# Windowed attention layers on one core: Q and K projected by column tiles and transposed on VectorE

## The chip, the cores and the metric

The kernel runs on one core of one Trainium2 chip. Its engines work side by side, each from its own queue in order: TensorE (PE; PEld is its weight load), VectorE (DVE), ScalarE (ACT), GpSimd (POOL), and SyncE (SP), which issues DMAs here. PE writes to the memory PSUM, in whose banks a tile here takes one or two; the other memory on the core is SBUF. The metric is device time in microseconds (us), lower is better. Two times differ by less than about 0.2% when they can't be told apart by the measurement.

## The reference, cut to what matters

A causal attention block stands first (4 sequences of 512 tokens, width 128, 16 heads of 64), then six layers of local attention, then one feed-forward block with the input of the layers added. The change is in the six layers. Per layer:

```python
q, k, v = jnp.split(x @ Wqkv, 3, -1)          # 16 heads of 64 each
q = l2norm(q) * qs                            # per token and head
k = l2norm(k) * ksc
q = q * cos * scale + rotate_half(q) * sin * scale
k = k * cos * inv + rotate_half(k) * sin * inv
out = local_attention(q, k, v)                # windows of 32, each sees itself and the one before
out = out.transpose(0, 2, 1, 3).reshape(b, n, INNER)
return out @ Wo
```

`rotate_half` swaps the two halves of a head's 64 columns and negates one. Each attention layer is followed by a feed-forward layer (layer norm, two products to 341, gelu gate, product back to 128). All in fp32.

## The kernel before, in words

**Stage one** (0 to about 540 us) is the dense causal attention; its functions are `make_q` to `residual1` (lines 260 to 401), its exponentials L339. The change leaves it alone but for the tables it prepares (`layer_tables`, L168).

**Stage two** is a pipeline over 96 units: 6 layers x 4 sequences x 4 tiles of 128 tokens (`Unit`, L530). One call of `slot(n, ...)` (L893) writes out, by hand and for all engines, the instructions of one step; each engine takes its own in that order. Slot n works on three units: u = n (scores to output), nxt = n+1 (transposes of Q and K) and new = n+2 (projections, rotation, norms). Every fourth slot begins the next sequence (`begin`, L847), and the feed-forward of a finished sequence (`Ffn`, L757) is spread over six slots: shift at n, mean, var and scale of its layer norm at n+1 to n+3, its three chunks with gelu at n+3 to n+5, its output product at n+6. So the slots repeat with period four. The steps that matter here:

- `project` (L535): the 128 tokens of the unit times the 1024 columns of Wq, Wk or Wv: two matmuls of 128x512 (four rows in the profile, since each fp32 matmul is two). Tokens stand on partitions, columns (head by head) along the free axis, in one of three PSUM tiles of two banks, `two0` to `two2`, which `two_t` (L516) hands out in rotation. In slot n Q's comes first, after the scores; K's in two halves; V's late.
- `square` (L549, ACT), `sum_squares` (L553, DVE): the sums of squares per token and head, 128x16 for Q and for K. `inverse_norms` (L580): a maximum with 1e-24 (L582), then `rsqrt` (L78): two integer operations on DVE for a first value (L84, L85) and three Newton steps of four operations on POOL (L87 to L90), on 128x32. `over_norm` (L585, POOL) multiplies Q and K by it.
- `rotate` (L558, DVE): the projection in PSUM times the cosine table (L561) and, with the halves swapped, times the sine table (L567); `add_rotated` (L577, POOL) adds the two.
- `transpose_q`, `transpose_k` (L654, L659): through `transposed` (L645), eight 128x128 PE transposes each into the two one-bank PSUM tiles of `one_t` (L520), copied out by ACT (L652). K's tile has 32 columns ahead of its 128, copied from the unit before by POOL (`carry_k`, L668), for the window that looks back.
- `scores` (L670): the mask as eight bf16 products in 64x32 tiles of PE (L676), then 64 products of 64x32 (L687). DVE takes the maximum over each head's 64 scores (L697) and subtracts it (L699); `exponents` (L703) is one ACT pass of 128x1024.
- `transpose_p`, `times_v` (L707, L712): eight PE transposes, two ACT copies, then 64 products with V (L719), whose extra column of ones gives the denominator; DVE divides (L728, L729). `transpose_o` and `project_out_2` (L736, L741) end the unit in the next slot.
- `v_windows` (L628): ACT copies V from PSUM (L634); SP stores it to DRAM and at once loads it back by windows (`vw`, L641).
- ACT holds one table of functions at a time: gelu needs another than the exponential, so a chunk's slot has a load before the gelu (L792) and one at the slot's end (L981).

Weights of the next layer (`wpart`, 512 KB each) are loaded after their last use (`do_project`, L859).

Of the kernel before, what the change touches and what calls it, by code (L numbers as in the profile page):

```python
# [32 lines left out]
def body(ctx: ExitStack, tc: tile.TileContext, a, out: bass.AP):  # L33
# [27 lines left out]
    hsel = const.tile([P, 2], F32, tag="hsel", name="hsel")  # L61
    nc.vector.memset(hsel, 0.0)
    nc.vector.memset(hsel[0:HD, 0:1], 1.0)
    nc.vector.memset(hsel[HD:P, 1:2], 1.0)
    tabs = const.tile([P, NT, 4, HD], F32, tag="tabs", name="tabs")
# [102 lines left out]
    def layer_tables(i):  # L168

        scales = pre.tile([P, 4 * HD], F32, tag="scales", name="scales")  # L170
        nc.sync.dma_start(out=scales, in_=a["scales"][i : i + 1].to_broadcast([P, 4 * HD]))
        lt = pre.tile([P, NT, 4, HD], F32, tag="lt", name="lt", bufs=2)
        nc.gpsimd.tensor_tensor(
            lt.rearrange("p t f d -> p t (f d)"),
            tabs.rearrange("p t f d -> p t (f d)"),
            scales.unsqueeze(1).to_broadcast([P, NT, 4 * HD]),
            ALU.mult,
        )
        return lt

    with tc.manual_schedule():
# [20 lines left out]
        nc.sync.dma_start(out=tabs, in_=a["tabs"])  # L202

# [209 lines left out]
        for m in range(last):  # L413
# [70 lines left out]
            if b == B - 1 and c == 2 and not odd:  # L484
                start = shifted(0), layer_tables(0)
# [4 lines left out]
    s2a = ps2a = s2b = s2 = ps_one = kT_first = vts = vds = None  # L490
# [44 lines left out]
    def project(u, j, c0=0, c1=2):  # L535
        p = u.p[j] if c0 else two_t(((1, 2, 1), (0, 2, 1), (1, 2, 0))[min(u.n, 2)][j], "ps_proj")
        u.p[j] = p
        for c in range(c0, c1):
            mm(  # L539
                p[:, c, :],  # L540
                lhsT=u.xs[:, u.T * P : (u.T + 1) * P],
                rhs=wpart[j][:, c * 512 : (c + 1) * 512],
                start=True,
                stop=True,
            )
        if c1 == 2:
            u.p[j] = flat(p)
# [4 lines left out]

    def sum_squares(u, j):  # L553
        if j == 0:
            u.ss = small.tile([P, 2 * HEADS], F32, tag="ss", name="ss")
        nc.vector.tensor_reduce(u.ss[:, j * HEADS : (j + 1) * HEADS], heads(u.sq[j]), AX.X, ALU.add)  # L556

    def rotate(u, j, between=()):  # L558
        t0 = u.r[j] = s2a.tile([P, INNER], F32, tag="rot", name="rot", bufs=6)
        lt, pf, half = u.lt, u.p[j], HD // 2  # L560
        nc.vector.tensor_tensor(  # L561
            heads(t0), heads(pf), lt[:, u.T, 2 * j].unsqueeze(1).to_broadcast([P, HEADS, HD]), ALU.mult
        )
        for f in between:
            f()
        t1 = u.t1 = s2a.tile([P, INNER], F32, tag="t1", name="t1", bufs=4)
        nc.vector.tensor_tensor(  # L567
            t1.rearrange("p (h t d) -> p h t d", t=2, d=half),
            pf.rearrange("p (h t d) -> p h t d", t=2, d=half)[:, :, ::-1, :],
            lt[:, u.T, 2 * j + 1]  # L570
            .rearrange("p (t d) -> p t d", t=2)
            .unsqueeze(1)
            .to_broadcast([P, HEADS, 2, half]),
            ALU.mult,
        )

    def add_rotated(u, j):  # L577
        nc.gpsimd.tensor_tensor(u.r[j], u.r[j], u.t1, ALU.add)  # L578

    def inverse_norms(u):  # L580

        nc.vector.tensor_scalar(u.ss, u.ss, 1e-24, None, ALU.max)  # L582
        rsqrt(u.ss, 2 * HEADS, nc.gpsimd)

    def over_norm(u, j):  # L585
        nc.gpsimd.tensor_tensor(  # L586
            heads(u.r[j]),
            heads(u.r[j]),
            u.ss[:, j * HEADS : (j + 1) * HEADS].unsqueeze(2).to_broadcast([P, HEADS, HD]),
            ALU.mult,  # L590
        )
# [8 lines left out]
    def second_step():  # L600

        nonlocal s2b, ps_one, kT_first, vts, vds
# [11 lines left out]
        kT_first = s2b.tile([P, NC, W + P], F32, tag="kT_first", name="kT_first")  # L614
        nc.gpsimd.memset(kT_first[:, :, 0:W], 0.0)
# [7 lines left out]
    def new_kT(u):  # L623
        if u.T == 0:
            return kT_first
        return s2.tile([P, NC, W + P], F32, tag="kT", name="kT", bufs=2)

    def v_windows(u):  # L628


        vt, vd = vts[u.n % 2], vds[u.n // NT % 2]
        src = u.p[2].rearrange("p (c a d) -> p a c d", a=2, d=HD)
        for c in range(2):
            nc.scalar.copy(vt[:, c, :, 0:HD], src[:, c])  # L634
        r0 = u.T * P
        nc.sync.dma_start(out=vd[r0 + W : r0 + W + P], in_=vt.rearrange("p a c d -> p a (c d)"))
        u.vw = s2b.tile([P, NW, NC, HD + 1], F32, tag="vw", name="vw", bufs=2)
        for odd in range(2):
            rows = vd[r0 + odd * W : r0 + odd * W + P].rearrange("(j k) a x -> a k j x", k=2 * W)
            for c in range(2):  # L640
                nc.sync.dma_start(  # L641
                    out=u.vw[c * HD : (c + 1) * HD, odd::2].rearrange("p j c d -> p j (c d)"), in_=rows[c]
                )
# [9 lines left out]

    def transpose_q(u):  # L654
        u.qT = s2b.tile([P, NC, P], F32, tag="qT", name="qT", bufs=1)
        for g in range(2):
            transposed(u.r[0], g, u.qT, 0)

    def transpose_k(u):  # L659
        if u.T == 0:  # L660
            u.kT = new_kT(u)
        for g in range(2):
            transposed(u.r[1], g, u.kT, W)

    def carry_k(u, nxt):
        if nxt is not None:
            nxt.kT = new_kT(nxt)
            nc.gpsimd.tensor_copy(nxt.kT[:, :, 0:W], u.kT[:, :, P : P + W])  # L668

    def scores(u):  # L670
# [13 lines left out]
        for c in range(NC):  # L684
            for j in range(NW):
                for h in range(2):
                    mm(  # L687
                        sc[j * W : (j + 1) * W, h, c * 2 * W : (c + 1) * 2 * W],
                        lhsT=u.qT[h * HD : (h + 1) * HD, c, j * W : (j + 1) * W],
                        rhs=u.kT[h * HD : (h + 1) * HD, c, j * W : (j + 2) * W],  # L690
# [4 lines left out]
        s3 = sc.rearrange("p a (c n) -> p a c n", n=2 * W)  # L695
        mx = small.tile([P, 2, NC], F32, tag="mx", name="mx")
        nc.vector.tensor_reduce(mx, s3, AX.X, ALU.max)  # L697
        u.pr = s2.tile([P, NC, 2, 2 * W], F32, tag="pr", name="pr", bufs=2)
        nc.vector.tensor_tensor(  # L699
            u.pr.rearrange("p c a n -> p a c n"), s3, mx.unsqueeze(3).to_broadcast([P, 2, NC, 2 * W]), ALU.subtract  # L700
        )

    def exponents(u):  # L703
        u.prf = u.pr.rearrange("p c a n -> p (c a n)")
        nc.scalar.activation(u.prf, u.prf, AF.Exp)
# [138 lines left out]
    def follower(u):  # L844
        return units[u.n + 1] if u.T + 1 < NT else None

    def begin(u):  # L847
# [3 lines left out]
        if u.n == 0:  # L851
            xs, lt = start
        else:
            xs = shifted(u.b)
            lt = layer_tables(u.i) if u.b == 0 else units[u.n - 1].lt
        for v in units[u.n : u.n + NT]:
            v.xs, v.lt, v.p = xs, lt, [None] * 3

    def do_project(u, j, c0=0, c1=2):  # L859
        project(u, j, c0, c1)  # L860
        if c1 == 2 and u.b + 1 == B and u.T + 1 == NT and u.i + 1 < L:
            wpart[j] = load_part(u.i + 1, j)

    def first_slot():
# [5 lines left out]
        do_project(new, 0)  # L870
        do_project(new, 1)
# [13 lines left out]
        inverse_norms(new)  # L885
        times_v1(B - 1, NC - 1, 1)
        second_step()
        over_norm(new, 0)
        over_norm(new, 1)
        do_project(new, 2)  # L890
        v_windows(new)

    def slot(n, norm, move, geglu):  # L893

        u, prev, nxt, new = unit(n), unit(n - 1), unit(n + 1), unit(n + 2)
        part[0] = -n % 3
        begin(unit(n + 4))  # L900
        if u:
            scores(u)
        if new:
            do_project(new, 0)
            square(new, 0)
        if u:
            exponents(u)
        while behind:
            behind.pop(0)()
# [3 lines left out]
        for f in norm:  # L913
            f()
# [4 lines left out]

        if new and n >= 0:  # L920
            rotate(new, 0, [lambda: residual(prev)] if prev else ())
            add_rotated(new, 0)
        elif prev:
            residual(prev)
        for f in move:
            f()
        if u and norm:
            transpose_p(u, 0)
        if new:
            do_project(new, 1, 0, 1)  # L930
        if u:
            if not norm:
                transpose_p(u, 0)
            transpose_p(u, 1)
        if new and n == -1:
            rotate(new, 0)
            add_rotated(new, 0)
        if new:
            do_project(new, 1, 1)
            square(new, 1)  # L940
        if n == -1:
            residual1(B - 1, y)
# [3 lines left out]
        while later:  # L946
            later.pop(0)()
        if new:
            sum_squares(new, 0)
# [3 lines left out]
        if nxt:  # L953
            transpose_q(nxt)
        if new:
            do_project(new, 2, 0, 2 if geglu else 1)
        if new and geglu:
            v_windows(new)
        if nxt:
            transpose_k(nxt)  # L960
        if new and not geglu:
            do_project(new, 2, 1)
            v_windows(new)
        if n == -1:
            third_step()
        if nxt:
            carry_k(nxt, follower(nxt))
        if new:
# [204 lines left out]
```

## Time and profile before

| | us |
|---|---|
| three runs | 2180.05, 2181.45, 2177.88; median 2180.05 |
| the profiled execution | 2177.22, of which its span 2175.2 |

The mean granted PE clock is 0.995 of full. Busy time in stretches of the span:

| us from the start | length | PE | DVE | ACT | POOL |
|---|---|---|---|---|---|
| 0 to 590 (stage one, start of stage two) | 590.0 | 570.1 | 389.0 | 353.5 | 296.0 |
| 590 to 1000 | 410.0 | 398.9 | 344.5 | 261.0 | 321.9 |
| 1000 to 1500 | 500.0 | 496.7 | 427.1 | 330.3 | 390.6 |
| 1500 to 2100 | 600.0 | 595.8 | 513.9 | 398.5 | 469.1 |
| 2100 to 2175 (end) | 75.0 | 65.5 | 45.6 | 37.5 | 30.7 |

Costliest groups of stage two, over the whole span (instructions, busy us, mean ns):

| line | what | count | busy | mean |
|---|---|---|---|---|
| L539 PE | projections, 128x512 | 1152 | 569.6 | 602 |
| L649 PE | transposes of Q and K, 128x128 | 1536 | 204.6 | 276 |
| L578 POOL | sum of the rotated parts, 128x1024 | 192 | 454.3 | 2367 |
| L586 POOL | product with the inverse norm, 128x1024 | 192 | 361.8 | 1905 |
| L561, L567, L556 DVE | rotation, sums of squares, 128x1024 | 192 each | 233.8, 233.2, 232.3 | 1217, 1215, 1210 |
| L551 ACT | squares, 128x1024 | 192 | 196.5 | 1024 |

How to read the profile: L539 is line 539 of the kernel. A row of a group has its count, then busy time and mean duration, then the engine's idle time just before the group and what ended most of it. In a timeline a row is start, duration (from the first start to the last end if several are merged, x8), engine, line, operation, output<-inputs; an idle time before it stands in brackets. A matmul's end is modelled and lies past the next one's start; `64*32` are the rows and columns of PE that it uses. "issue" is a wait for nothing that the profile shows.

### The profile page before, as it was taken

The page shows a single profiled execution, that of the slowest core. Times are in us where ns is not written, and L with a number is a line of the kernel's source. Part 1 is how long each engine was busy: PE and PEld are TensorE (multiplying, and loading weights), DVE is VectorE, ACT ScalarE, POOL GpSimd, SP SyncE. Part 2 cuts the span into 40 slices and gives each one's busy share as a digit, 9 for nine tenths or more (in the row PEclk, how much of TensorE's full clock was granted, in tenths as well). Part 3 has the DMA queues.
Part 4 walks back from the last instruction along what each step waited for, and adds up shares of the span by engine and source line. Part 5 has one row for each costly group of instructions (what it writes and reads, how often), then busy time and mean ns, then how long its engine had stood idle before and what let it go on. Part 6 is the DMA issues. An engine that isn't in the chain of part 4 may idle for free.

```text
span 2175.2 us, 80486 instructions
## 1 busy us (share of the span) xinstructions
PE 2127.0 (98%) x35150; PEld 1424.5 (65%) x35150; DVE 1720.1 (79%) x2501; ACT 1380.8 (63%) x2677; POOL 1508.3 (69%) x2279
## 2 busy tenths in 40 slices
PE   7999999999999999999999999999999999999998
PEld 5655656555566666676667666666766676667665
DVE  3776766767778888888888888888888888888884
ACT  3675656755455667666676666676666666666764
POOL 2554545455787787777877877877877778778773
PEclk8999999999999999999999999999999999999999
DMA  3000000000343353343434334433453344434331
GB/s 126 1 1 1 1 1 1 1 1 1 100 111 99 99 135 101 101 114 99 120 111 109 102 100 128 116 91 111 106 136 92 101 119 112 115 103 114 91 101 41
DMA packets 88812, 180.17 MB, mean 83 GB/s; under 512 B 9327, under 2 KB 23405, under 8 KB 88429
## 3 DMA queue, kind: packets, MB, share of 16 engines
q1 hardware_dynamic: 87756, 173.31, 29.3%
q8 instruction: 278, 4.55, 0.9%
q10 hardware_dynamic: 704, 1.70, 0.2%
q14 instruction: 74, 0.60, 0.1%
HBM read 122.81 MB, written 52.43 MB: 81 GB/s over the span
## 4 chain that ended last, share of the span: by engine, by line
PE 87%; DVE 9%; POOL 1%; ACT 1%; issue 1%; DMA 0%; SPq 0%; DVEq 0%; POOLq 0%; ACTq 0%
PE ps_proj L539 21%; PE ps_one L649 15%; PE ps_one L744 7%; PE ps_att L719 6%; PE ps_sc L299 6%; PE ps_att L687 5%; PE ps_o L384 5%; PE ps_pt L364 5%; PE ps_proj L808 3%; PE ps_proj L788 2%; PE ps_proj L789 2%; PE ps_pj L278 1%; PE ps_att L676 1%; DVE ss L556 1%; PE ps_pj L268 1%; DVE ss L582 1%
## 5 line engine op out<-in xcount | busy, mean ns | idle before, releaser
L578 POOL TENSOR_TENSOR rot<-rot,t 128x1024 f32<-128x1024 f32 x192 | 454.3, 2367 | 176.2 <-DVE t L567 161.4
L539 PE MATMUL ps_proj<-wqkv,xs 128*128 128x512 f32 x1152 | 569.6, 602 | 0.2
L353 POOL TENSOR_TENSOR pr<-pr,den 128x1024 f32<-128x1024 f32 x128 | 240.9, 1892 | 248.9 <-DVE den L350 239.0
L586 POOL TENSOR_TENSOR rot<-rot,ss 128x1024 f32<-128x1024 f32 x192 | 361.8, 1905 | 7.4
L551 ACT ACTIVATE sq<-ps_proj 128x1024 f32<-128x1024 f32 x192 | 196.5, 1024 | 172.4 <-PE ps_proj L539 145.0
L539 PEld LDWEIGHTS ps_proj<-wqkv,xs 128*128 128x128 f32 x1152 | 188.5, 190 | 102.9 <-issue 93.8
L561 DVE TENSOR_TENSOR rot<-ps_proj,lt 128x1024 f32<-128x1024 f32 x192 | 233.8, 1217 | 6.0 <-ACT sq L551 5.2
L567 DVE TENSOR_TENSOR t<-ps_proj,lt 128x1024 f32<-128x1024 f32 x192 | 233.2, 1215 | 0.0
L556 DVE TENSOR_REDUCE ss<-sq 128x16 f32<-128x1024 f32 x192 | 232.3, 1210 | 0.0
L339 ACT ACTIVATE pr<-ps_sc,nm 128x128 f32<-128x128 f32 (+3 forms) x448 | 220.3, 509 | 11.8 <-DVE nm L326 8.6
L649 PEld LDWEIGHTS ps_one<-ident,rot 128*128 128x128 f32 x1536 | 171.6, 141 | 66.9 <-issue 43.3
L649 PE MATMUL ps_one<-ident,rot 128*128 128x128 f32 x1536 | 204.6, 276 | 5.2 <-POOL rot L586 4.5
L326 DVE TENSOR_REDUCE nm<-ps_sc 128x2 f32<-128x1024 f32 x128 | 156.0, 1219 | 64.6 <-PE ps_sc L314 64.5
L744 PEld LDWEIGHTS ps_one<-aT,wo 128*128 128x128 f32 x1536 | 182.9, 192 | 23.7 <-issue 23.0
L652 ACT COPY pT<-ps_one 128x512 f32<-128x512 f32 x192 | 110.1, 586 | 136.5 <-PE ps_one L649 136.4
L744 PE MATMUL ps_one<-aT,wo 128*128 128x128 f32 x1536 | 189.2, 276 | 0.4 <-DVE rs L114 0.3
L719 PEld LDWEIGHTS ps_att<-vw,pT 64*32 64x32 f32 x12288 | 130.9, 105 | 77.0 <-ACT pT L652 69.0
L728 DVE RECIPROCAL rden<-ps_att 128x8 f32<-128x8 f32 x192 | 39.0, 203 | 174.0 <-PE ps_att L719 173.9
L634 ACT COPY vt<-ps_proj 128x512 f32<-128x512 f32 x192 | 103.2, 590 | 97.2 <-PE ps_proj L539 90.9
L652 ACT COPY qT<-ps_one 128x512 f32<-128x512 f32 x192 | 103.1, 589 | 96.0 <-PE ps_one L649 96.0
L87 POOL TENSOR_TENSOR yt<-y 128x32 f32<-128x32 f32 (+2 forms) x384 | 87.7, 228 | 108.0 <-DVE y L85 62.0
L364 PEld LDWEIGHTS ps_pt<-ident,pr 128*128 128x128 f32 x1024 | 117.2, 141 | 58.5 <-issue 47.7
(171 smaller groups left out, 4164.2 us busy)
## 6 DMA issues: line engine op xcount, KB each, us to landing
vw<-vd SPq DMA_DIRECT2D x384, 260.0 KB, 4.9
vd<-vt SPq DMA_DIRECT2D x96, 520.0 KB, 2.7
wqkv<-in_wqkv_dram SPq DMA_DIRECT2D x18, 512.0 KB, 4.9
wo<-in_wo_dram SPq DMA_DIRECT2D x6, 512.0 KB, 7.2
w<-in_w_dram SPq DMA_DIRECT2D x6, 341.0 KB, 6.3
xr<-in_x_dram SPq DMA_DIRECT2D x3, 256.0 KB, 7.4
scales<-in_scales_dram SPq DMA_DIRECT2D x6, 128.0 KB, 4.5
w<-in_w_dram SPq DMA_DIRECT2D x12, 64.0 KB, 5.5
```

The source lines that it names most:

```text
L339: nc.scalar.activation(self.pr[:, h, cols], self.sc[:, h, cols], AF.Exp, bias=self.nm[:, part_, h : h + 1], accum_out=self.den[:, part_, h ...
L353: nc.gpsimd.tensor_tensor(self.pr, self.pr, self.den[:, 0].unsqueeze(2).to_broadcast([P, 2, S]), ALU.mult)
L364: nc.tensor.transpose(pt[:, k * P : (k + 1) * P], self.pr[:, h, k * P : (k + 1) * P], ident)
L539: mm(p[:, c, :], lhsT=u.xs[:, u.T * P : (u.T + 1) * P], rhs=wpart[j][:, c * 512 : (c + 1) * 512], start=True, stop=True,)
L556: nc.vector.tensor_reduce(u.ss[:, j * HEADS : (j + 1) * HEADS], heads(u.sq[j]), AX.X, ALU.add)
L561: nc.vector.tensor_tensor(heads(t0), heads(pf), lt[:, u.T, 2 * j].unsqueeze(1).to_broadcast([P, HEADS, HD]), ALU.mult)
L567: nc.vector.tensor_tensor(t1.rearrange("p (h t d) -> p h t d", t=2, d=half), pf.rearrange("p (h t d) -> p h t d", t=2, d=half)[:, :, ::-1, :],
L578: nc.gpsimd.tensor_tensor(u.r[j], u.r[j], u.t1, ALU.add)
L586: nc.gpsimd.tensor_tensor(heads(u.r[j]), heads(u.r[j]), u.ss[:, j * HEADS : (j + 1) * HEADS].unsqueeze(2).to_broadcast([P, HEADS, HD]), AL ...
L649: nc.tensor.transpose(tp[:, c * P : (c + 1) * P], src[:, (4 * g + c) * P : (4 * g + c + 1) * P], ident)
L719: mm(o[j * W : (j + 1) * W, h, c * (HD + 1) : (c + 1) * (HD + 1)], lhsT=u.pT[h * HD : (h + 1) * HD, 4 * g + c, j * W : (j + 1) * W], rhs=u ...
L744: mm(y[:, 0:P], lhsT=wo_w[0][:, c, :], rhs=u.aT[:, c, :], start=(c == 0), stop=(c == NC - 1))
```

## The change

1. **Columns and tiles of the Q and K projection.** The host permutes the columns of Wq and Wk: the 1024 are four blocks of 256, block b holding, for each of the 8 pairs of heads, 32 of a head's 64 columns. `project` makes, per window of 32 tokens and per block, one product of 32 tokens x 256 columns, put on partitions 32b to 32b+31: 16 products of 128 rows x 32 columns of PE for each of Q and K. So a partition now stands for (block, token of the window), the free axis for (window, pair of heads, 32 columns).
2. **Transposes.** In that layout the 32x32 blocks need only be transposed each in place: one DVE transpose of 128x1024 for Q and one for K, straight into `qT` and `kT` in SBUF. The PE transposes and ACT copies of Q and K are gone. The halves that the rotation exchanges lie in one partition's block of 32, so `rotate` multiplies without a swap and `add_rotated` reads one operand with the halves exchanged.
3. **Norms.** A head's 64 columns lie on two partitions, so the sums (128x32 for Q and for K now) are added over pairs of partitions by a product with a 0/1 matrix (`pair_sums`, into a one-bank tile). DVE guards against zero; ACT gives a first value as exp(-0.5 ln v); POOL makes one Newton step.
4. **Exponentials.** The subtraction on DVE is gone: the maximum is taken negated, and ACT makes 16 exponentials of 128x64 from PSUM with it as bias, eight before and eight after the seed of the norms.
5. **Order.** The Q projection is done for unit n+3 at the slot's end, in place of n+2 after the scores; norms and transposes for n+1 come a slot after its projection; V's projection goes through the one-bank tiles; V's windows are loaded a slot after they are stored. The second half of K's projection stands before the second transposes of the probabilities, not after. Loading the exponential's table is a plain load of the set that has logarithm and exponential.
6. Tables: per token and block, built per tile on POOL (`layer_table`).

```diff
+    def project(u, j, p, c0=0, c1=2):
+        for w_ in range(2 * c0, 2 * c1):
+            t0, n = u.T * P + w_ * W, NC * W
+            for b_ in range(4):
+                mm(
+                    u.p[j][b_ * W : (b_ + 1) * W, w_ // 2, w_ % 2 * n : (w_ % 2 + 1) * n],
+                    lhsT=u.xs[:, t0 : t0 + W],
+                    rhs=wpart[j][:, b_ * n : (b_ + 1) * n],
+                    start=True,
+                    stop=True,
+                )
...
     def add_rotated(u, j):
-        nc.gpsimd.tensor_tensor(u.r[j], u.r[j], u.t1, ALU.add)
+        r, t1 = (x_.rearrange("p (g t d) -> p g t d", t=2, d=W // 2) for x_ in (u.r[j], u.t1))
+        nc.gpsimd.tensor_tensor(r, r, t1[:, :, ::-1], ALU.add)
...
-        rsqrt(u.ss, 2 * HEADS, nc.gpsimd)
+    def pair_sums(u):
+        u.pair = one_t()[:, 0 : 2 * GROUPS]
+        mm(u.pair, lhsT=pairs, rhs=u.ss, start=True, stop=True)
+    def guard(u):
+        u.v = small.tile([P, 2 * GROUPS], F32, tag="v", name="v")
+        nc.vector.tensor_scalar(u.v, u.pair, 1e-24, None, ALU.max)
+    def seed(u):
+        u.y = small.tile([P, 2 * GROUPS], F32, tag="y", name="y")
+        nc.scalar.activation(u.y, u.v, AF.Ln, scale=float(1 << 16))
+        nc.scalar.activation(u.y, u.y, AF.Exp, scale=-0.5)
+    def newton(u):
+        v, y, eng = u.v, u.y, nc.gpsimd
+        t = small.tile([P, 2 * GROUPS], F32, tag="yt", name="yt")
+        eng.tensor_tensor(t, y, y, ALU.mult)
+        eng.tensor_tensor(t, t, v, ALU.mult)
+        eng.tensor_scalar(t, t, -0.5 * (1 << 24), 1.5 * (1 << 8), ALU.mult, ALU.add)
+        eng.tensor_tensor(v, y, t, ALU.mult)
...
+    def transpose_q(u):
+        u.qT = s2b.tile([P, NW, NC, W], F32, tag="qT", name="qT", bufs=1)
+        nc.vector.transpose(out=u.qT.rearrange("p w c d -> p (w c d)"), in_=u.r[0])
+    def transpose_k(u):
+        u.kT = s2b.tile([P, NW + 1, NC, W], F32, tag="kT", name="kT", bufs=2)
...
+            nc.gpsimd.tensor_copy(u.kT[:, 0], units[u.n - 1].kT[:, NW])
+        nc.vector.transpose(out=u.kT[:, 1:].rearrange("p w c d -> p (w c d)"), in_=u.r[1])
...
-        nc.vector.tensor_reduce(mx, s3, AX.X, ALU.max)
...
+        nc.vector.tensor_reduce(u.mx, s3, AX.X, ALU.max, negate=True)
+    def exponents(u, g):
...
+        for c in range(4 * g, 4 * g + 4):
+            for h in range(2):
+                nc.scalar.activation(
+                    u.pr[:, c, h], u.sc[:, h, c * 2 * W : (c + 1) * 2 * W], AF.Exp, bias=u.mx[:, h, c : c + 1]
+                )
```

The new order of a slot, with what each step is for (u = n, done = n+1, new = n+2, newq = n+3, prev = n-1):

```python
load_v(done); scores(u); pair_sums(done); begin(unit(n + 4)); maximum(u); guard(done)
exponents(u, 0); seed(done); exponents(u, 1)
project_out_2(prev); rotate(new, 0, [residual(prev)])
# norm and move steps of the feed-forward
newton(done); over_norm(done, 0); over_norm(done, 1)
sum_squares(new, 0); add_rotated(new, 0)
project(new, 1, k_tile, 0, 1); transpose_p(u, 0); project(new, 1, k_tile, 1); transpose_p(u, 1)
square(new, 1); times_v(u, 0); times_v(u, 1)
# later steps of the feed-forward's norm
transpose_q(done); transpose_k(done)
rotate(new, 1); add_rotated(new, 1); sum_squares(new, 1); project_v(new)
# geglu: chunk or output product of the feed-forward
project(newq, 0, q_tile); preload_act_table_set(...); square(newq, 0); transpose_o(u)
```

`q_tile` is the slot's `two0`, the tile that its scores had; `k_tile` is `two2`, which the next slot's scores take.

## The prediction

> **What bounds the kernel now.** I read the page first (busy times and the chain that ended last), then the timeline of TensorE (PE) over single units, then the groups by form.
>
> ```profile
> PE 2127.0 (98%) x35150; PEld 1424.5 (65%) x35150; DVE 1720.1 (79%) x2501; ACT 1380.8 (63%) x2677; POOL 1508.3 (69%) x2279
> ...
> PE 87%; DVE 9%; POOL 1%; ACT 1%; issue 1%; DMA 0%; SPq 0%; DVEq 0%; POOLq 0%; ACTq 0%
> ```
>
> PE is 98% busy and 87% of the chain, so its work is the time. One unit (128 tokens of one layer) in the timeline, PE's rows alone:
>
> ```profile
> 1356.32 0.41 PE L676 MATMUL ps_att<-band,ident 64*32 64x512 bf16 x8
> 1356.54 1.41 PE L687 MATMUL ps_att<-kT_first,qT 64*32 64x64 f32 x122
> 1358.85 0.31 PE L687 MATMUL ps_att<-kT_first,qT 64*32 64x64 f32 x6 [0.90 <-issue]
> 1359.09 1.98 PE L539 MATMUL ps_proj<-wqkv,xs 128*128 128x512 f32 x4
> ...
> 1362.69 1.02 PE L539 MATMUL ps_proj<-wqkv,xs 128*128 128x512 f32 x2
> ...
> 1363.55 1.04 PE L649 MATMUL ps_one<-ident,pr 128*128 128x128 f32 x8
> ...
> 1365.38 1.51 PE L719 MATMUL ps_att<-vw,pT 64*32 64x65 f32 x128
> ...
> 1369.47 1.04 PE L649 MATMUL ps_one<-ident,rot 128*128 128x128 f32 x8
> ...
> 1373.03 0.41 PE L676 MATMUL ps_att<-band,ident 64*32 64x512 bf16 x8
> ```
>
> Starts tell the pace, since ends are modelled: a 512-column product (two rows, x2) takes 0.86 us (1362.69 to 1363.55), a 128x128 transpose 0.107. From mask product (L676) to mask product is one slot. Over the span the slots repeat by four: 15.7, 16.75, 17.4 and 16.2 us, mean 16.51; the long ones carry the feed-forward's mean and its second product. Between groups of equal tile shape PE loses nothing (within 4 ns at the common boundaries); wherever the tile shape changes (128*128 to 64*32 or back) the next start comes 92 to 94 ns late, each time. PE has no slack to give, the others have.
>
> **PE after the change.** Per unit it loses the 16 transposes of Q and K: 16 x 0.1075 = 1.72. It gains the pair-sum product (two short rows behind two weight loads, 0.21 by L112's eight in 0.79) and six more changes of shape (ten for four, as the K projection in halves now stands between 128*128 groups): 0.56. The projections keep their columns: 16 products of 256 columns in four column tiles are as long as two of 512 if the four tiles run together. The trace has this in two near forms: 8 tiles of 64*32 (L719, 128 rows in 1.51 us, where one after the other 65 columns at 0.84 ns would take 7.0), and two column tiles that use all 128 rows:
>
> ```profile
> 336.56 1.94 PE L384 MATMUL ps_o<-pT,v 128*64 128x512 f32 x8
> ```
>
> Eight rows of 512 columns in the time of L539's four. So I take 1.72 per projection, and bound it by 1.72 and, with only two tiles at once, 3.44. Sum: -1.72 + 0.21 + 0.56 = -0.95, which makes PE alone 14.75, 15.8, 16.45, 15.25.
>
> [...] L384's loads share all row groups with the running products and cost no gap. [...]
>
> **The circle that may replace PE.** Before, scores are followed by maximum and subtraction (1.22 each) and one exponential (1.05), with 2.6 us of Q projection and more on PE meanwhile. After, the Q projection stands at the slot's end, and ScalarE (ACT) does 16 exponentials of 64 columns with a bias from SBUF. No row shows 64 columns; stage one has the same form from 128 up:
>
> ```profile
> 319.33 0.37 ACT L339 ACTIVATE pr<-ps_sc,nm 128x128 f32<-128x128 f32 x1
> 319.60 0.20 ACT L339 ACTIVATION_READ_ACCUMULATOR pr<-ps_sc,nm 128x1 f32 x1
> 319.69 0.37 ACT L339 ACTIVATE pr<-ps_sc,nm 128x128 f32<-128x128 f32 x1
> 319.94 0.21 ACT L339 ACTIVATION_READ_ACCUMULATOR pr<-ps_sc,nm 128x1 f32 x1
> ```
>
> 128 columns start 0.250 before the next instruction, 256 columns 0.357: 0.83 ns a column, so 64 columns 0.196 apart; I take 0.20, and 0.32 for the last of a series. Bounds: 0.09 (a read of the accumulator to the next start) and 0.32 (no overlap).
>
> [...]
>
> From the end of the score stream: maximum starts at 0.2 (L697 starts 0.25 after the last score row starts) and ends at 1.42; eight exponentials to 3.18 (0.04 to start, 7 x 0.20 + 0.32); logarithm and exponential of the seeds (64 columns, 0.2 each) to 3.5; eight more to 5.2; second transposes of the probabilities at 5.25, the first copy (0.59) done at 5.7, times_v 5.8 to 7.3. PE's own work up to that transpose is only 4.5 to 5.3 us, so it waits 0 to 0.8. From 7.3 on PE is full: V 1.72, feed-forward chunk 1.72 (its second product 2.58 in every fourth slot), Q of the third next unit 1.72, transposes of the output 0.86, mask and scores 1.75, four changes of shape 0.36. The circle closes at 15.43 (16.29 in the fourth). With PE's own sums the slots become 15.43, 15.8, 16.45, 15.43, mean 15.78: **0.73 us less than 16.51**.
>
> **The other engines.** VectorE (DVE) loses the subtraction (1.22), the 32-column maximum L582 and the two bit operations of the seed (0.47), and gains a guard (about 0.2) and two 32x32-block transposes of 128x1024, which no row shows.
>
> ```profile
> L697 DVE TENSOR_REDUCE mx<-ps_att 128x16 f32<-128x1024 f32 x30 | 36.5, 1217 | 5.9 <-PE ps_att L687 5.6
> ...
> L582 DVE TENSOR_SCALAR ss<-ss 128x32 f32<-128x32 f32 x30 | 43.1, 1436 | 1.0
> ```
>
> Every DVE pass over 128x1024 takes 1.21 to 1.23, from PSUM or SBUF; I take 1.2. Below: 1.09 (twice L126's 547 ns for 512). Above: 2.4, which is 1.2 and the stall that L582 shows (1.4 us beside a working GpSimd, 0.17 at 565.17 with GpSimd idle), or GpSimd's own pass (L578, 2.37). Its circle: times_v ends at 7.3, the last normalisation at 8.45, both transposes at 10.8, K's two rotations (they free the bank that the next mask needs) at 13.1, scores end at 14.9. So 0.5 us per slot hides it, up to 1.46 us a transpose. GpSimd (POOL) does four steps of 64 columns instead of twelve of 32: seeds at 3.5, one refinement at 4.75 (0.31 apart, as L87 to L90 follow each other now), both products by 1.9 at 8.6, before the K transpose would start (9.6); later than that adds to DVE's circle. Before it come only the shifts of every fourth slot (two of 1.3, which use up the 1 us there). ACT gains 16 x 0.20 + 0.3 and loses 1.05 and four copies (about 2.2 net of overlap); in feed-forward slots it ends its queue (copies of V, table load 1.28, gelu 0.69, table load 1.28, square 1.02, two copies) at 15.35, just before the next output projection wants the copies at 15.75. One more table load falls in the slots without gelu, where ACT is free by two microseconds. SP issues the V window loads one slot after the store and one before their use (4.9 us to landing); the next layer's Q weights still have a slot. Hidden, all of it; if ACT slips by over 0.4, PE waits for the rest.
>
> **Sum.** The stage is 96 units; the last ones project nothing new, so 92 x 0.73 = 67 less. The last unit's exponentials are exposed (16 x 0.20 for 1.22 + 1.05): +1. The smaller tables in stage one: +1 on a half-idle POOL. The profiled execution took 2177.2 us (span 2175.2), so 2112; the runs' median is 2.8 higher: **2115 us**.
>
> **Rivals.** (a) The circle is shorter than laid out and PE alone is left (mean 15.56): 92 x 0.95 = 87 less, 2093; PE's fullness today speaks for it, the exposed waits in the layout against. [...] (c) Slower: the transposes take DVE's long form, 2.4 us each. DVE's circle is then 17.3 and becomes the slot: 92 x 0.8 = 75 more, 2257. It decides from 1.95 us each on, where its mean circle reaches 16.51. For it: L582's stalls; against: the one-source pass L556 shows no stall beside POOL. (d) The four tiles do not run together, so the change does not do what it says: 3.44 per projection, PE 19.0, 92 x 2.5 = 230 more, 2410.
>
> **Chances.** Forecast (2090 to 2145) 0.57; (a) 0.08; (b) 0.13, split 0.06 faster, 0.05 same, 0.02 slower; (c) 0.12; (d) 0.05; something unseen 0.05, half on either side. About 0.2% is what a measurement here can tell from no change. Faster 0.75, same 0.05, slower 0.20. The range 2075 to 2200 holds the forecast, (a), (b) and the mild end of (c), about 8 in 10.
>
> **What would show it.** Right: the Q and K projection in 1.7 to 1.9 us each by starts; block transposes near 1.2; exponentials 0.20 apart; PE waiting up to 0.8 before the second transposes of the probabilities; slots of 15.4 to 16.5. Wrong: the next mask waiting for K's rotation (DVE's circle), exponentials further apart, or a projection row count that takes over 2 us.

## The result, and the profile after

The changed kernel takes 2251.36 us (median of four runs, 2242.71 to 2257.68) where the kernel before takes 2180.41: the ratio is 1.0325, 95% interval 1.0287 to 1.0362. It is slower; 2115 us and "faster" were forecast. The profiled execution took 2257.68 us, its span 2255.9.

The page of the changed kernel, first the engines' busy time, then a queue and two groups, last the chain:

```profile
PE 2108.4 (93%) x39182; PEld 1338.7 (59%) x39182; DVE 1705.3 (76%) x2402; ACT 1457.2 (65%) x3860; POOL 1374.0 (61%) x1582
...
q8 instruction: 309, 5.06, 1.0%
...
PE 78%; DVE 11%; ACT 5%; issue 4%; POOL 1%; DMA 0%; SPq 0%; DVEq 0%; ACTq 0%; POOLq 0%
...
L743 ACT ACTIVATE pr<-ps_att,mx 128x64 f32<-128x64 f32 x1536 | 333.1, 328 | 202.9 <-DVE mx L735 202.9
L547 PE MATMUL ps_proj<-wqkv,xs 128*32 128x256 f32 x6144 | 399.3, 388 | 4.9 <-DVE t L602 2.5
```

TensorE is busy for 19 us less than before (the prediction's sum for TensorE alone takes 92 x 0.95 = 87 us away), but only 93% of a longer span. No other engine has filled up: all are below 77%. So TensorE waits, and the chain gives 4% to "issue" (1% before), time in which an engine waited for nothing that the profile shows. Its longest waits (us in total, times, longest):

```profile
PE ps_att L759 <- issue: 40.5, 34, 1.7
PE ps_att L711 <- DVE t L602: 21.9, 19, 4.0
PE ps_one L784 <- issue: 17.7, 10, 3.1
```

Two slots from TensorE's timeline show where. A slow one, 18.63 us from mask (L711) to mask:

```profile
1001.29 0.41 PE L711 MATMUL ps_att<-band,ident 64*32 64x512 bf16 x8
...
1003.26 2.00 PE L784 MATMUL ps_one<-aT,wo 128*128 128x128 f32 x16
1006.47 1.02 PE L100 MATMUL ps_one<-tmp_t,avg 128*128 128x512 f32 x2 [1.20 <-DVE xT L792]
...
1010.59 1.17 PE L759 MATMUL ps_att<-vw,pT 64*32 64x65 f32 x85
1012.79 0.68 PE L759 MATMUL ps_att<-vw,pT 64*32 64x65 f32 x43 [1.03 <-issue]
1013.40 1.98 PE L562 MATMUL ps_one<-wqkv,xs 128*128 128x512 f32 x4
...
1019.92 0.41 PE L711 MATMUL ps_att<-band,ident 64*32 64x512 bf16 x8
```

and an undisturbed one, 15.37 us (the first of a group of four, the slow one is a second; undisturbed second slots take 15.9 to 16.2):

```profile
1128.54 0.41 PE L711 MATMUL ps_att<-band,ident 64*32 64x512 bf16 x8
...
1135.95 1.51 PE L759 MATMUL ps_att<-vw,pT 64*32 64x65 f32 x128
1137.39 1.98 PE L562 MATMUL ps_one<-wqkv,xs 128*128 128x512 f32 x4
...
1143.91 0.41 PE L711 MATMUL ps_att<-band,ident 64*32 64x512 bf16 x8
```

In the slow slot times_v stops after 85 of its 128 products, in the middle of a group whose operands are all there, and goes on a microsecond later. In the other slot the same group is one line. The 1.20 us ahead of L100 are a pause of the same kind, though the profile names VectorE's xT (L792) as the releaser: in the undisturbed slot from 1143.91 L100 starts at 1147.64, before L792 does (1148.11), so it does not need it. Slow slots come in stretches of eight or nine (16.8 to 21.9 us each), with as many undisturbed ones (15.4 to 17.8) between, about once per layer.

**What the pauses have in common** is a count. The instruction queue (q8) moved 309 packets of 16,384 bytes, 5.06 MB; TensorE's records (a weight load, a product and a semaphore instruction are one each) are 79,097, so an instruction is 64 bytes and a packet 256 of them: this queue carries TensorE's program. If TensorE's records are numbered in order from 0, all 45 pauses inside a group that are over 0.9 us from start to start, in layers and tail, end at number 193 or 194 modulo 256: they stand where one block of 256 instructions of the program ends and the next begins (the records start 62 instructions into one). In each a packet of this queue has started within the pause or up to 1.8 us ahead of it, and TensorE goes on 2.2 to 3.0 us after the packet's start: at 1010.40 a packet starts, lasts 0.96 us, and 2.39 us after its start TensorE goes on. The wait ahead of L100 ends at number 193 too, 2.65 us after a packet's start. Counted at block beginnings alone, from 540 us to the end, TensorE starts over 0.8 us after the product before it 56 times in the changed kernel (92.6 us together) and 10 times in the kernel before (11.1 us). These times run from start to start, and some hold another engine's wait as well.

A group of four slots has 3013 instructions, 59 short of 12 blocks, so the place in the slot at which a block begins moves by 59 instructions per four slots, and is back where it was after some 17 slots. Mean slot of the units 8 to 91 by that place, counted in instructions from the mask (two more blocks begin 256 and 512 instructions later):

```
first block begins at      16-59   60-103  104-155  156-199  200-255   0-15
changed kernel, us         19.40   18.14   17.53    16.20    16.32     16.60
kernel before, us          16.61   16.94   16.39    16.57    16.59     17.16
```

The changed kernel depends on the place by over 3 us; the kernel before varies by 0.8 us, with its longest slots in the last column, which has five slots.

### The profile page after: what moved, and what is told of

It is laid out like the page before. It is cut to its first block, busy times and chain, and to the rows that moved or that the text cites. A ratio compares the mean times of both kernels' runs of the same rounds, so it can differ in the third digit from the quotient of the medians.

```text
span 2255.9 us, 88566 instructions
## 1 busy us (share of the span) xinstructions
PE 2108.4 (93%) x39182; PEld 1338.7 (59%) x39182; DVE 1705.3 (76%) x2402; ACT 1457.2 (65%) x3860; POOL 1374.0 (61%) x1582
## 3 DMA queue, kind: packets, MB, share of 16 engines
q8 instruction: 309, 5.06, 1.0%
## 4 chain that ended last, share of the span: by engine, by line
PE 78%; DVE 11%; ACT 5%; issue 4%; POOL 1%; DMA 0%; SPq 0%; DVEq 0%; ACTq 0%; POOLq 0%
PE ps_proj L547 13%; PE ps_one L700 7%; PE ps_one L784 6%; PE ps_att L759 6%; PE ps_att L722 6%; PE ps_one L562 6%; PE ps_sc L303 5%; PE ps_o L388 5%; PE ps_pt L368 4%; ACT pr L743 3%; PE ps_proj L828 3%; PE ps_proj L829 3%; DVE mx L735 2%; PE ps_att L711 1%; PE ps_proj L848 1%
## 5 line engine op out<-in xcount | busy, mean ns | idle before, releaser
L743 ACT ACTIVATE pr<-ps_att,mx 128x64 f32<-128x64 f32 x1536 | 333.1, 328 | 202.9 <-DVE mx L735 202.9
L547 PE MATMUL ps_proj<-wqkv,xs 128*32 128x256 f32 x6144 | 399.3, 388 | 4.9 <-DVE t L602 2.5
L640 POOL TENSOR_TENSOR rot<-rot,v 128x1024 f32<-128x1024 f32 x192 | 363.2, 1913 | 7.5
L547 PEld LDWEIGHTS ps_proj<-wqkv,xs 128*32 128x32 f32 x6144 | 172.5, 110 | 211.0 <-issue 120.0
L602 DVE TENSOR_TENSOR t<-ps_proj,lt 128x1024 f32<-128x1024 f32 x192 | 232.4, 1210 | 0.0
L596 DVE TENSOR_REDUCE ss<-sq 128x32 f32<-128x1024 f32 x192 | 231.2, 1204 | 0.0
L602 DVE TENSOR_TENSOR rot<-ps_proj,lt 128x1024 f32<-128x1024 f32 x192 | 230.2, 1199 | 0.0
L569 ACT COPY vt<-ps_one 128x512 f32<-128x512 f32 x192 | 113.3, 590 | 180.7 <-PE ps_one L562 180.7
L784 PE MATMUL ps_one<-aT,wo 128*128 128x128 f32 x1536 | 201.8, 285 | 17.9 <-issue 17.7
L759 PE MATMUL ps_att<-vw,pT 64*32 64x65 f32 x12288 | 160.0, 225 | 44.2 <-issue 40.5
L784 PEld LDWEIGHTS ps_one<-aT,wo 128*128 128x128 f32 x1536 | 186.8, 198 | 19.6 <-issue 19.3
L562 PE MATMUL ps_one<-wqkv,xs 128*128 128x512 f32 x384 | 192.2, 622 | 6.5 <-DVE aT L398 3.6
L634 POOL TENSOR_TENSOR yt<-y 128x64 f32<-128x64 f32 x96 | 28.0, 292 | 241.6 <-ACT y L629 239.7
L735 DVE TENSOR_REDUCE mx<-ps_att 128x16 f32<-128x1024 f32 x96 | 117.5, 1224 | 75.6 <-PE ps_att L722 75.2
```

Of the source, the lines that this page charges most:

```text
L547: mm(u.p[j][b_ * W : (b_ + 1) * W, w_ // 2, w_ % 2 * n : (w_ % 2 + 1) * n], lhsT=u.xs[:, t0 : t0 + W], rhs=wpart[j][:, b_ * n : (b_ + 1) * n],
L562: mm(p, lhsT=u.xs[:, u.T * P : (u.T + 1) * P], rhs=wpart[2][:, g * 512 : (g + 1) * 512], start=True, stop=True,)
L596: nc.vector.tensor_reduce(u.ss[:, j * GROUPS : (j + 1) * GROUPS], groups(u.sq[j]), AX.X, ALU.add)
L602: nc.vector.tensor_tensor(out_.rearrange("p (w c d) -> p w c d", w=NW, d=W), u.p[j].rearrange("p (w c d) -> p w c d", w=NW, d=W), lts[u.T] ...
L640: nc.gpsimd.tensor_tensor(groups(u.r[j]), groups(u.r[j]), u.v[:, j * GROUPS : (j + 1) * GROUPS].unsqueeze(2).to_broadcast([P, GROUPS, W]), ...
L743: nc.scalar.activation(u.pr[:, c, h], u.sc[:, h, c * 2 * W : (c + 1) * 2 * W], AF.Exp, bias=u.mx[:, h, c : c + 1])
```

## The experiments

The theory from here on: TensorE waits for its own program. It runs through 256 instructions of the scores or of times_v in 1.5 to 1.6 us, and a block cannot be had that fast (in e6_micro below, one took 3.45 to 4.0 us). The rivals: the slow stretches belong to the change of layer (weight loads, tables), or to the clock, which was lowered in some of them. The edits are shown shortened.

**Locking the places.** e1_lock_good adds products of one column that are overwritten at once, some before the stage and 29 in every fourth slot, so that four slots have 12 x 256 instructions. e2_lock_bad differs in the number before the stage alone.

```diff
+        if u.n == 0 and j == 0:
+            for k in range(95):                    # e2_lock_bad: 25
+                mm(u.p[j][0:W, k % 2, 0:1], lhsT=ident16[...], rhs=ident16[..., 0:1], start=True, stop=True)
...
+        if u.T == 3 and u.n < 92:
+            for k in range({3: 49, 7: 47}.get(u.n, 29)):
+                mm(sc[j * W : (j + 1) * W, h, 0:1], lhsT=ident16[...], rhs=band[rows, 1, 0:1], start=True, stop=False)
```

> The changed kernel with one-column bf16 products (two instructions each, written and overwritten, no result changes) in TensorE's stream: 95 once before the stage, then 49, 47 and from there 29 ahead of the mask of every fourth unit. They bring four slots from 3013 to 3072 = 12 x 256 instructions, so that the 256-instruction blocks in which TensorE's program is fetched begin at the same places of every slot, and at places (172 to 235 instructions into the slot, and 256 and 512 later) where the changed kernel's trace shows no pause. Theory (the pauses are TensorE waiting for its own program): no pause over 0.8 us between products of one line in the layers, every group of four slots at 15.5, 16.1, 16.9 and 16.6 us plus about 0.35 for the extra products, mean 16.4 against 17.22 in the changed kernel: 93 x 0.85 = 79 us less, 2178 us. Rival 1 (the pauses come with the change of layer, its weight loads and tables): the slow stretches stand where they stood, 93 x 0.1 = 10 us more, 2262 us. Rival 2 (the lowered clock makes the slots slow): the same as rival 1, as the extra products keep TensorE no busier than before.

> The same as e1_lock_good with 25 instead of 95 one-column products before the stage, 140 instructions fewer in all, nothing else changed: the blocks now begin 55 to 120 instructions into every slot, and 256 and 512 later, where the changed kernel's trace has its pauses. Theory (TensorE waits for its own program): every slot is a slow one; the changed kernel's slots at these places took 18.3, 19.3, 17.4 and 18.7 us, mean 18.4, so 93 x 1.2 = 112 us more than the changed kernel, 2370 us (2330 to 2420), with one or two pauses of 1.2 to 2 us in each slot. Both rivals (change of layer, clock): as they expect of e1_lock_good, 2262 us, since the two kernels differ in 70 one-column products of about 12 ns.

Measured: e1_lock_good 2167.38 us, ratio to the kernel before 0.9943 (0.9927 to 0.9959); e2_lock_bad 2325.68 us, 1.0662 (1.0644 to 1.0679). From their pages, TensorE's busy time and times_v's group (last column: idle time before its products):

```profile
PE 2082.4 (96%) x39982; PEld 1327.7 (61%) x39982; DVE 1711.4 (79%) x2402; ACT 1456.3 (67%) x3860; POOL 1377.6 (64%) x1582
...
L776 PE MATMUL ps_att<-vw,pT 64*32 64x65 f32 x12288 | 151.7, 225 | 4.6 <-ACT pT L708 0.9
```

```profile
PE 2121.4 (91%) x39912; PEld 1340.3 (58%) x39912; DVE 1689.0 (73%) x2402; ACT 1458.2 (63%) x3860; POOL 1371.5 (59%) x1582
...
L776 PE MATMUL ps_att<-vw,pT 64*32 64x65 f32 x12288 | 172.8, 224 | 118.3 <-issue 117.9
```

70 one-column products decide over 158 us. In e1_lock_good 7 block beginnings are late (10.8 us; five of them are a pause in the scores, which the theory had not expected at these places), in e2_lock_bad 124 (179.4 us, 91 of them in times_v). Both rivals expected 2262 for both. The clock goes the other way besides: between the first mask and the last it is lowered for 44 us in the changed kernel, for 27 in the slower e2_lock_bad. Against the expectation e1_lock_good is 11 us lower and e2_lock_bad 44: its slots took 17.9 us, not 18.4.

**Shifting the places** by half a block, once:

```diff
+        if u.n == 0 and j == 0:
+            for k in range(64):
+                mm(u.p[j][0:W, k % 2, 0:1], lhsT=ident16[...], rhs=ident16[..., 0:1], start=True, stop=True)
```

> The changed kernel with 64 one-column products (128 instructions, half a block) once before the stage and nothing else. In the changed kernel a block begins 18 to 155 instructions into the slots of units 5 to 13, 22 to 31, 40 to 48, 57 to 66, 75 to 83, and these are the slow ones; with the shift they are units 0 to 5, 13 to 22, 31 to 39, 48 to 56, 65 to 75 and 84 to 92. Theory (TensorE waits for its own program): the slow stretches move by half their period to these units, fast ones in between, and the time stays within 2230 to 2300 us (55 slow units for 49, some 6 x 1.8 = 11 us more, 2268). Rivals (change of layer, clock): the slow stretches stay at the units where they were, 2258 us.

Measured: 2264.5 us, 1.0373 (1.0349 to 1.0397). The 37 units from 8 to 91 that were slow in the changed kernel and should be freed fell from 18.37 us to 16.37; the 40 that should become slow rose from 16.34 to 18.19. The stretches follow the count of instructions, not the layers.

**The fetch by itself.** Runs of 1536 instructions, of which only the columns differ:

```diff
+            for n in (32, 64, 96, 128, 192):
+                for k in range(384):
+                    mm(u.p[j][q * W : (q + 1) * W, h, 0:n], lhsT=ident[rows, 0:W], rhs=flat_t[rows, 0:n], start=True, stop=True)
```

> The changed kernel with five runs of 384 fp32 products (1536 instructions, six blocks of 256) over the eight tiles of 64x32 before the stage, with 32, 64, 96, 128 and 192 columns; they are written and overwritten, and 7680 instructions are 30 whole blocks, so the layers keep their places. At 12.1 ns for a product pass of 64 columns and its weights (L722) a block of 256 instructions would take 0.8, 1.55, 2.3, 3.1 and 4.65 us. Theory (a block cannot begin before its fetch has ended, and the fetch can start only a limited number of instructions ahead): the runs of 32 and 64 columns, and perhaps 96, go at one pace, that of the fetch, 2.2 us or more for a block, with a pause at each block; the wide ones go at their own pace without pauses. Rival (the pauses belong to waits around the runs and not to the fetch): every run goes at its own pace, 1.55 us for 256 instructions at 64 columns.

Measured: 2360.64 us in a single run, 109 more than the changed kernel; 30 blocks at 3.67 us are 110. From its timeline, one or two lines of each width (128 products with their weight loads are one block):

```profile
542.37 1.54 PE L550 MATMUL ps_proj<-tabs,ident 64*32 64x32 f32 x128 [2.45 <-issue]
...
564.46 2.04 PE L550 MATMUL ps_proj<-tabs,ident 64*32 64x64 f32 x128 [1.41 <-issue]
...
590.29 1.72 PE L550 MATMUL ps_proj<-tabs,ident 64*32 64x96 f32 x128 [2.01 <-issue]
594.01 1.72 PE L550 MATMUL ps_proj<-tabs,ident 64*32 64x96 f32 x128 [2.01 <-issue]
...
608.65 2.02 PE L550 MATMUL ps_proj<-tabs,ident 64*32 64x128 f32 x128 [1.00 <-issue]
...
623.57 2.83 PE L550 MATMUL ps_proj<-tabs,ident 64*32 64x192 f32 x128 [1.50 <-issue]
627.02 2.83 PE L550 MATMUL ps_proj<-tabs,ident 64*32 64x192 f32 x128 [0.62 <-issue]
```

All five runs go at one pace: the 30 blocks begin 3.45 to 4.0 us apart, 3.67 on the average, from 32 to 192 columns, at a granted clock of 0.5 (51 us of these 109) as at full clock. No other DMA packet starts meanwhile, so it is not traffic that slows the fetch here. The pace is that of the fetch, and two thirds longer than the 2.2 us that was expected at least. Even products of 192 columns did not hide it. For these the expectation had it wrong: it laid out 4.65 us for a block, longer than a fetch, and they take 2.83; so no run here was slow enough to go without pauses.

**Time without instructions.** If a block is late because its predecessor was used up too fast, then added work of few instructions costs little where it gives the fetch time. e8_bad_spread is e2_lock_bad with two products of 128x512 in every slot:

```diff
+        for k in range(2):          # first transposes of the probabilities only
+            mm(tp, lhsT=ident, rhs=tabs.rearrange("p a b c -> p (a b c)")[:, 0:512], start=True, stop=True)
...
-            for k in range({3: 49, 7: 47}.get(u.n, 29)):
+            for k in range({3: 37, 7: 33}.get(u.n, 15)):
```

> e2_lock_bad with two more products of 128x512 (0.86 us each, eight instructions, written and overwritten) ahead of the first transposes of the probabilities in every slot, and 15 instead of 29 one-column products in every fourth, so that the places of the blocks stay locked within a few instructions (57 to 103 into the slot). TensorE has 1.72 us more work in every slot between the scores and times_v, and next to no more instructions. Theory (a pause comes where 256 instructions are used up faster than the next block comes): the added time lets the fetch catch up, the pauses in times_v (91 of them, about 1.5 us each in e2_lock_bad) mostly go, and the added 160 us of work cost 40 us or less: 2326 to 2366 us. Rival (the pauses are a fixed cost of a block that begins at these places): 93 x 1.72 = 160 us more, 2480 us.

Measured: 2355.33 us, 1.0808 (1.0776 to 1.0841): 160 us of work for 30 us of time. Its TensorE's longest waits:

```profile
PE ps_proj L552 <- issue: 29.2, 40, 1.7
PE ps_one L117 <- issue: 11.7, 9, 2.2
```

The 91 pauses in times_v are down to one; of late block beginnings 42 are left (54.2 us), and all but two of them lie ahead of the added work, at K's projection and at the norm's transposes.

**VectorE's stall.** In every fourth slot the next mask came late even where no pause disturbed it, after 17.6 to 17.8 us. VectorE's and GpSimd's timeline there:

```profile
1170.40 0.18 DVE L81 TENSOR_SCALAR yt<-rs 128x4 int32<-128x4 int32 x1
1170.52 2.35 POOL L614 TENSOR_TENSOR rot<-rot,t 128x1024 f32<-128x1024 f32 x1
1170.62 2.28 DVE L82 TENSOR_SCALAR y<-yt 128x4 int32<-128x4 int32 x1
...
1172.81 1.23 DVE L677 STREAM_TRANSPOSE qT<-rot 128x1024 f32<-128x1024 f32 x1
...
1173.97 1.20 DVE L685 STREAM_TRANSPOSE kT<-rot 128x1024 f32<-128x1024 f32 x1
...
1175.10 1.18 DVE L602 TENSOR_TENSOR rot<-ps_proj,lt 128x1024 f32<-128x1024 f32 x1
...
1176.20 1.20 DVE L602 TENSOR_TENSOR t<-ps_proj,lt 128x1024 f32<-128x1024 f32 x1
```

L82, four columns wide, ends with GpSimd's pass (at 1172.90 and 1172.87), and both transposes and K's rotation queue behind it. e4_actseed takes the two seed operations from VectorE:

```diff
+        if seed:
+            nc.scalar.activation(y, v, AF.Ln)
+            nc.scalar.activation(y, y, AF.Exp, scale=-0.5)
+        else:
             nc.vector.tensor_scalar(ti, v.bitcast(I32), 1, None, ALU.logical_shift_right)
             nc.vector.tensor_scalar(y.bitcast(I32), ti, -1.0, 1597463007.0, ALU.mult, ALU.add)
```

> The changed kernel with the seed of the feed-forward norm's reciprocal root (two int32 operations of 4 columns on VectorE, the second 2.28 us long in the trace because it ends only with GpSimd's pass) taken by a logarithm and an exponential on ScalarE, 0.26 us each. TensorE's instructions stay as they are. Theory (in every fourth slot VectorE's queue, with this stall in it, releases the next mask product late): these slots fall from 17.65 (16.9 between weight loads) by 1.2 to 1.6 us, 23 x 1.2 to 1.6 = 28 to 37 less, about 2225 us; the slow stretches stay where they are. Rival (ScalarE's two more operations and the queue behind them, copies of V and the gelu, become the bound of these slots): no gain, 2255 to 2265.

Measured: 2245.46 us, 1.0299 (1.0277 to 1.0321), 6 us below the changed kernel and not 28 to 37; the two intervals overlap, so it may be no gain. The theory held for half of these slots: of the 21 among the units 8 to 91 the ten undisturbed ones fell from 17.67 to 16.79 us (medians), the eleven in the slow stretches did not (18.24 and 18.54). There the pauses of the fetch seem to take the gain.

**Both together**, with the blocks 16 instructions earlier:

> e1_lock_good and e4_actseed together, with 8 more one-column products before the stage, so that the blocks begin 16 instructions earlier in every slot (156 to 221 instead of 172 to 237). Theory (two separate costs: TensorE waiting for its program, and VectorE's seed held up by GpSimd's pass): e1_lock_good's 2167 us less the seed's 1.0 us in each group of four slots (in e4_actseed four undisturbed slots took 64.0 us together, in the changed kernel 65.0), 24 us, less the one pause of 1.3 us per layer that e1_lock_good kept inside the scores, 8 us: 2135 us (2125 to 2148). Rival (ScalarE's longer queue takes back what VectorE saves, as the mere 6 us of e4_actseed could mean): 2158 to 2165 us.

Measured: 2153.43 us, 0.9879 (0.9855 to 0.9902): faster than both kernels, 14 us below e1_lock_good, but 18 above the expectation. TensorE is now 97% busy (page):

```profile
PE 2084.6 (97%) x39990; PEld 1330.7 (62%) x39990; DVE 1660.1 (77%) x2358; ACT 1461.0 (68%) x3904; POOL 1374.4 (64%) x1582
```

The slot with the stall fell from 17.80 to 16.97 us (medians), and the three others rose by 0.03 to 0.18; so 0.54 us are left of each group of four. The pause in the scores stayed, one in five of the six layers (1.0 to 1.4 us from start to start, at a block's beginning): the 16 instructions did not move it out of the way, and why it comes in that unit of each layer stays open.

**The tail.** The changed kernel's end after the last mask takes 49.2 us, before 40.9.

```diff
+        for k in range(keep):       # 4, ahead of the last unit's mask
+            mm(sc[:, k % 2, :], lhsT=ident, rhs=tabs.rearrange("p a b c -> p (a b c)")[:, 0:512], start=True, stop=True)
```

> e5_best with four products of 128x512 (0.86 us each, written and overwritten) ahead of the last unit's mask, in the 4.1 us in which TensorE has nothing to do before the last scores. In the changed kernel a lowered clock (0.5) follows this gap, for 13.7 us (10.2 in e1_lock_good), and the end after the last mask takes 49.2 us against 40.9 in the kernel before. Theory (the clock is lowered because TensorE stood idle): with the gap filled no lowered clock is granted before the last microseconds, and the time is 4 to 6 us below e5_best. Rival (the tail is longer because the last unit's products on GpSimd and its two transposes stand between the last slot and its scores, whatever the clock): within 1 us of e5_best.

Measured: 2154.18 us, 0.9879 (0.9854 to 0.9905), no gain. Between the mask before the last and the last microseconds the lowered clock went from 13.7 to 3.4 us, but from that mask to the end the kernel takes 61.0 us for 61.2. So the clock doesn't make the tail; that the chain of products, two transposes and scores does is what is left, and was not tried by itself.

## Why the prediction was wrong

**The step that failed** is the one called "PE after the change". It adds up times of rows: "The projections keep their columns: 16 products of 256 columns in four column tiles are as long as two of 512 if the four tiles run together". They do run together (Q's takes 1.77 us by starts without the change of shape behind it), and they take eight times the instructions: 32 products and 32 weight loads per projection for 4 and 4. A slot went from 671 to 753 instructions on the average, and the sum put them at nothing. In their place the runs show the 92.6 us at block beginnings, and 84 us between the changed kernel and e1_lock_good, which has the same work (and its one-column products) with the blocks elsewhere. None of the rivals had this; it falls under the 0.05 for "something unseen". The average rate would still do (753 in 16.2 us, when e6_micro shows 256 in 3.67), but not where they are dense. From the first score product to the last of times_v the kernel before has about 579 instructions in 9.8 us, an undisturbed slot of the changed kernel 631 in 8.9; at 3.67 us per 256 the fetch needs 8.3 and 9.0 (an estimate from e6_micro's pace). The shorter circle, which was the gain, brought the two dense runs together until they outran the fetch; e8_bad_spread takes them apart again, and the pauses in times_v go. How much the added instructions do without the shorter way, and the other way round, was not tried. The kernel before's profile had a sign of it, in a line that the prediction itself shows: the scores of its slot are split into x122 and x6 by 0.90 us "<-issue". It was quoted as pace and not asked about; it stands at a block's beginning, and ends 2.35 us after a packet's start.

**What the 146 us between forecast and profiled run (2112 and 2258) are made of:** 92 in the layers' slots go with e1_lock_good, fetch and lowered clock together; 12 more with e5_best, VectorE's stall; 16 are head and tail; the remaining 26 are the undisturbed slots, 16.08 us in e5_best (mean of the four medians) where 15.78 were laid out.

**The lowered clock** is part of the first term. After a pause of 3.83 us the sixteen products of L784 take 3.73 us, not 2.00:

```profile
962.95 1.46 PE L722 MATMUL ps_att<-kT,qT 64*32 64x64 f32 x128
968.24 0.69 PE L620 MATMUL ps_one<-ss,pairs 128*128 128x64 f32 x2 [3.83 <-ACT pr L743]
968.73 3.73 PE L784 MATMUL ps_one<-aT,wo 128*128 128x128 f32 x16
```

The releaser named had nothing to do with it (L743 runs only after the maximum): the product at 968.24 opens a block. The granted clock is 0.5 for 6.8 us from 966.5 on, and ten times in the layers for 44 us in all; the kernel before has 3.4. At half speed that is at most 22 us (an estimate, half of the 44). The ten come in or right after pauses of TensorE of 1.7 to 4.0 us.

**The circle through ACT was right.** Exponentials are 0.20 apart (eight take 1.72 to 1.75 us), and the undisturbed first slot takes 15.4 to 15.6 for the 15.43 laid out.

**The block transposes were right**: 1.233 and 1.201 us for the 1.2 taken. Rival (c), whose 2257 us is near the result, is wrong none the less: it needed 2.4 us each.

**"So 0.5 us per slot hides it" was wrong in every fourth slot**: the two seed operations stand in front of the transposes there, and VectorE's circle of that slot was laid out without them. It is the stall that the prediction had read off L582 and applied to the transposes alone. The term of 0.5 us is 2.4 short there, of which 0.83 us showed in the slot.

**PE alone** was 0.2, 0.4 and 0.7 us short in the second, third and fourth slot (15.99, 16.86 and 15.95 in e5_best, where TensorE has hardly a gap in them, for 15.8, 16.45 and 15.25; the third is without the 0.11 us of its added products). The projections explain 0.15 of it: 1.86 us by starts with the change of shape behind them (0.09), and 1.00 for each half of K's, for 1.72 without. The rest was not followed up.

**Head and tail** were laid out at 1 us each; the head took 10 us more and the tail 8. The first mask stands at 571.0 for 561.0 (stage one ends 2.6 us later, then TensorE waits 3.6 us for DVE's aT with nothing else to do and 3.1 for the first rotation of K, with a lowered clock after the first); in the tail the last unit's products on GpSimd and its two transposes have no work of another unit beside them.

Rivals (a), (b) and (d) did not come: the exponentials are exposed as laid out, the longer step that (b) counts on is shown by no run (they are 0.20 us apart), and the tiles run together (1.77 us for Q's projection).

## What to carry to other kernels

Count instructions beside microseconds: TensorE's program came at a pace of its own here (256 instructions in 3.67 us in e6_micro), and stretches that used it up faster (256 instructions of the scores or of times_v in 1.5 to 1.6 us) stopped at places that depended on everything issued before: 70 one-column products ahead of the stage decided between 7 late block beginnings (e1_lock_good) and 124 (e2_lock_bad). A pause inside a group whose operands are ready, with "issue" as its releaser, is worth a count modulo the block (256 instructions here). When a change splits products into smaller ones and also shortens the way between two dense runs, add up both; and take a quoted wait that nothing explains as a question, not as noise.

## What the runs showed of the hardware that was not expected

- In e6_micro TensorE gets 256 instructions (64 bytes each) per 3.45 to 4.0 us in an unbroken run, 14.3 ns an instruction on the average, whether its products have 32 columns or 192. The least time from one packet's start to the next is 3.30 us in the kernel before, 3.32 in the changed kernel and 3.24 in all ten traces. The scores of the changed kernel use up an instruction in 6.1 ns (256 in 1.55 us).
- A packet of the fetch lasts 0.88 to 2.0 us (0.88 to 1.84 in the changed kernel), and no block begins less than 2.16 us after its packet's start (2.18 in the changed kernel). What sets the moment at which a fetch starts (it was 1 to 301 instructions ahead of the block's first, 1 to 298 in the changed kernel) was not found out.
- In the changed kernel an int32 TENSOR_SCALAR of four columns on VectorE took 2.28 us beside a GpSimd TENSOR_TENSOR and ended with it (1172.90 and 1172.87); with GpSimd idle (2231.43 in the tail, three columns) it took 0.17.
- A VectorE transpose in blocks of 32x32 of 128x1024 fp32 took 1.20 to 1.25 us in the changed kernel, where the other passes over 128x1024 took 1.20 to 1.22 on the average (L602, L596, L735).
